# Layer 0 of a fused four-layer network: result slots, weight sets in four pairs, statistics of layer 1 ahead, sums later

## The chip, the cores and the metric

The kernel runs on one core of one Trainium2 chip. The metric is device time in microseconds. The kernel before took 2876.43 us (median of 3 runs, 2876.21 to 2878.43). The engines are named as in the profile: PE is TensorE's matmul, PEld its weight load, DVE is VectorE, ACT is ScalarE, POOL is GpSimd, SP is SyncE. SP and POOL issue almost all transfers here. [...]

## The reference

The input is 1024 images of 16 x 16 points with 16 channels, in fp32. Four layers follow one another, each of the form `x = x + f(gn(x))`, with a group norm of 8 groups of 2 channels over all points of an image:

```python
x = x + _L0_conv_ref(_gn(x), core0, core1, core2)          # tensor-train matrix of 4096 x 4096
x = x + _L1_conv_ref(_gn(x), conv1, conv2, fc0, fc1, 1)    # cellular automaton step
x = x + _L2_conv_ref(_gn(x), filters, bias)                # 3 x 3 convolution
x = x + _L3_conv_ref(_gn(x), ...)                          # a second automaton step
```

Layer 0 multiplies each image, taken as a vector of 4096, by a matrix that three small cores define. In a step of the automaton, a depthwise pair of 3 x 3 filters and the channels themselves go through two dense layers (48 to 128, ReLU, 128 to 16); a mask from 3 x 3 maxima of one channel is applied. The group norm needs, for each image and group, a mean, a variance and one over its root.

## The kernel before, in words

The batch is handled as two chunks of 512 images. Two large tiles in SBUF, `XN[0]` and `XN[1]` (names in the trace: xn), each of 128 partitions x 16384 values, hold what is being worked on. Images and results between layers stand in DRAM: `xf` is the running x of a chunk by channel and line, `xr` the raw input by line, `xb` normed blocks.

**Layer 0** is a matrix product of 4 x 4 blocks with two chunks, computed by a table of 26 outer products (`OUTER`), taken in 13 pairs, numbered 0 to 12 here (called phases in the code). A pair has 4 units (one for each quarter q of the output), so that there are 52 units. A unit has 7 inner products (`INNER`) in two half-steps each, 14 steps of 4 matmuls of 128 x 256 (L1482). Pair p works on tile `XN[p % 2]`: X in columns 0 to 8191 and three combined sums E in 8192 to 14335, both read by all its units. Around the matmuls a unit has: `build` of the weights of the next unit (matmuls L1386, copies by ACT L1391), sums of weights by DVE (`mix`, L1416), ACT copies of the first results into a result tile r (L1524, L1526) and DVE adds into it (L1518, L1528), and `store` of the unit before, at step 1: results that are added in DRAM go through POOL with an accumulating transfer (L1459), the first ones through SP (L1461). For r, units 0 to 3 and the later odd ones use one buffer (`r`), the later even ones the end of `XN[0]`.

Beside each pair run other steps, spread over the pair's steps by a small planner (`run`): a list of (cost, step) entries and of pauses, with a start and an end as shares of the pair. An entry gets its due place from the costs and pauses before it, and is emitted behind the step of the pair that has reached this place. So the planner only sets the order on each engine; nothing in it waits for a clock. These are:

- `part_steps(j)` (L1160 to L1240): loads, four of 1 MB on SP, and sums for pair j, beside pair j - 1. Pieces of 512 KB go through a ring of four buffers (`t4`), fetched two ahead. The same ring serves negated results (`neg`).
- `combined(j)` (L1131): ten DVE operations that make pair j's sums E and change X. They stand at the end of pair j - 1, or, for pairs in `late` (1, 4, 6), between the first steps of pair j itself.
- The two sets of weights of the automaton steps, `nca_weights` (L262 to L404), in columns 8192 to 14335 of `XN[0]`, beside pairs 3 and 5: many small transfers on POOL, small matmuls (L287 to L311), zero fills, and then 11 folds: `make` is four small matmuls (L392) and four ACT copies (L398) into one of three buffers, `send` stores that buffer in DRAM in small pieces, half of them on SP and half on POOL (L404).
- `residual_steps` (L1266): 32 accumulating transfers of 512 KB, raw input into `xf`, on POOL, beside pairs 4 to 9.
- The convolution's weights, beside pair 7.
- `mean_ahead` (L900 to L916), beside pair 10: the means of layer 1's norm for chunk 0, from pieces of `xf` by DVE sums (L903), a matmul over channels, an ACT copy and a store to `means`.

Beside pair 12 the result of layer 0 for chunk 0 is loaded into `XN[1]` and normed there: means are loaded and subtracted (L727), squares (ACT L712) are summed (DVE L694), a matmul gives the variance (L862), roots follow for three quarters (L767 to L778), a matmul spreads them (L874), and DVE multiplies. The last quarter is finished beside the first half of layer 1 (`layer_nca`, PE lines L1889 and L1718).

Of the kernel before, what the change touches and what calls it, by code (L numbers as in the profile page):

```python
# [10 lines left out]
F32 = mybir.dt.float32  # L11
# [10 lines left out]
P = 128  # L22
# [83 lines left out]
def conv_preact_kernel(ctx: ExitStack, tc: tile.TileContext, a: dict, out: bass.AP):  # L106
# [121 lines left out]
    def nca_weights(pre, room):  # L228
# [6 lines left out]
        L["pack"] = dram.tile([P, 833], F32, tag=pre + "pk", name=pre + "pk")  # L235

# [79 lines left out]
        def xpats():  # L316
            xw = pk[:, 0:512].rearrange("p (n k) -> p n k", n=4)
            for n, pat in enumerate(XPATS):
                for v, s in enumerate(pat):
                    if s is not None:  # L320
                        G.dma_start(xw[16 * v : 16 * v + 16, n], fz[s, 1 : S + 1])
            for g in range(1, 4):
                G.dma_start(pk[32 * g : 32 * g + 32, 0:513], pk[0:32, 0:513])
            G.dma_start(L["pack"], pk)

# [43 lines left out]
        def fold(n):  # L369

            steps = []
            for f in range(2):
# [38 lines left out]
                steps += [make, send]  # L411
            return steps

        steps = [inputs, dense0, bias_lines, bias_rows, dense1, taps, order, xpats]
        return L, steps + [x for n in range(len(TERMS)) for x in fold(n)]


# [401 lines left out]
    def paced(parts, st):  # L819

        def begin():
            st["t"], st["q"] = parts[0](), parts[1]()

        def add():
            V.tensor_tensor(st["t"], st["t"], st["q"], ALU.add)

        def last():
            st["s"] = work([P, NB], "s", "s2s")  # L830
            V.tensor_tensor(st["s"], st["t"][:, 0], st["t"][:, 1], ALU.add)

        steps = [(2, begin), (1.2, add)]
        for part in parts[2:]:
            steps += [1.5, (1, lambda part=part: st.update(q=part())), (1.2, add)]
        return steps + [(0.8, last)]

    def parts_cw(X, on_act, paced_from=4):
# [3 lines left out]
        for q in range(4):  # L842
# [6 lines left out]
            if q < paced_from:  # L849
                N["sq"].append(centred(subs, more2))  # L850
            else:
                s2.clear()
                N["sq"].append(subs + paced(squares(X, l0, 8, on_act), s2))
# [31 lines left out]
    def alone(N, q):  # L885

        return (
            N["sums"][q] + [3, N["mean"][q], 1, N["held"][q], 1] + N["sq"][q]
            + [3, N["var"][q], 1, N["keep"][q]]
        )  # L890

    means = dram.tile([4, P, NB], F32, tag="means", name="means")

    def mean_ahead(q):

        st = {}

# [3 lines left out]

        def add(w):
            V.tensor_tensor(st[0], st[0], st[w], ALU.add)  # L903

        def last():
            st["s"] = work([P, NB], "s", "s1s")
            V.tensor_tensor(st["s"], st[0][:, 0], st[0][:, 1], ALU.add)
# [5 lines left out]
        def keep():  # L913
            st["m"] = work([P, NB], "s", "m")
            A.copy(st["m"], st["p"])
            nc.sync.dma_start(means[q], st["m"])  # L916

        steps = [(0, lambda: load(0)), (0, lambda: load(2)), 4]
        for w in (2, 4, 6):
            if w < 6:  # L920
                steps.append((0, lambda w=w: load(w + 2)))
            steps.append((1.2, lambda w=w: add(w)))
        return steps + [(0.8, last), 2, (0.6, mean), 1, (0, keep)]

    def apart(N, q):

        def mean():
            N["st"]["m", q] = work([P, NB], "s", "m")
            nc.sync.dma_start(N["st"]["m", q], means[q])

        return [(0, mean), 3] + N["sq"][q] + [5, N["var"][q], 1, N["keep"][q]]
# [213 lines left out]
    def part_steps(j):  # L1145
# [25 lines left out]

# [34 lines left out]
        if todo:  # L1206
            steps += [(0, lambda: fetch(0)), (0, lambda: fetch(1)), 3]
# [909 lines left out]
```

## Time and profile before

| what | value |
|---|---|
| median of the runs | 2876.43 us |
| the profiled execution | 2877.63 us, of which the span of its instructions 2875.9 us |
| PE / DVE / ACT / POOL busy | 2722.2 / 1987.6 / 1267.0 / 510.7 us |
| layer 0, pairs 0 to 12 | 46.9 to 1678.4 us |
| pair 3, pair 5 | 148.4 us, 160.2 us |
| pair 7, pair 9 | 108.4 us, 114.3 us |
| pair 10, 11, 12 | 115.8, 107.2, 123.8 us |
| layer 1, first and second chunk | 244.6 us, 237.0 us |

Times in the trace count from the start of the span. In a table of stretches each row is one stretch, with its length, the busy time and the instruction count of each engine, the granted TensorE clock as a share, the busy share of the 16 DMA engines, and GB/s. In a list of waits a row names the engine and line that waited, whom it waited for, the total in us, how often, and the longest. In groups of instructions a row has the busy time, the mean of one in ns, and the idle time ahead of them.

### The profile page before, as it was taken

How to read it: one execution, taken by the hardware profiler on the slowest of the kernel's cores; microseconds unless marked ns; L12 is line 12 of the kernel's file. 1: busy time of each engine (PE TensorE's matmuls, PEld its weight loads, DVE VectorE, ACT ScalarE, POOL GpSimd, SP SyncE). 2: the span in 40 equal slices, each digit the busy share in tenths (PEclk: the TensorE clock that was granted, in tenths of full speed). 3: DMA queues.
4: the chain of work that ended last, by engine and by line, in shares of the span. 5: the costliest groups of instructions: out<-in, count | busy, mean ns of one | idle time of the engine just before them, and what ended most of it. 6: DMA issues, size and time to landing. Idle time of an engine off the chain costs nothing.

```text
span 2875.9 us, 48113 instructions
## 1 busy us (share of the span) xinstructions
PE 2722.2 (95%) x19342; PEld 1776.3 (62%) x19342; DVE 1987.6 (69%) x2420; ACT 1267.0 (44%) x2140; POOL 510.7 (18%) x662
## 2 busy tenths in 40 slices
PE   6888899799979999999999999999999999999997
PEld 5677788578757888888888743333333333334444
DVE  8476667666747867756666788857877776766654
ACT  3223322242233222222222346666778657676664
POOL 2000012642452142121011011111112221110000
PEclk8989999899989999999999999999999999999998
DMA  6566576899888788897667365455566867454665
GB/s 249 175 222 251 192 211 147 198 222 186 217 178 215 173 183 190 191 227 186 167 173 187 76 160 105 96 128 154 108 145 137 190 101 195 101 101 104 172 176 202
DMA packets 254558, 488.29 MB, mean 170 GB/s; under 512 B 28708, under 2 KB 96344, under 8 KB 245120
## 3 DMA queue, kind: packets, MB, share of 16 engines
q1 hardware_dynamic: 172240, 328.16, 34.7%
q0 software_dynamic: 81904, 156.93, 32.2%
q8 instruction: 153, 2.51, 0.3%
q14 instruction: 69, 0.57, 0.1%
q10 hardware_dynamic: 192, 0.13, 0.0%
HBM read 268.98 MB, written 221.11 MB: 170 GB/s over the span
## 4 chain that ended last, share of the span: by engine, by line
PE 78%; DVE 7%; DMA 7%; issue 2%; POOL 2%; ACT 1%; SPq 1%; DVEq 0%; ACTq 0%; POOLq 0%
PE po L1482 36%; PE ph L1889 20%; PE po L1718 8%; PE po L1573 5%; PE pw L1386 5%; DMA xf<-r 1%; DMA xn<-in_x_dram 1%; DMA L_conv_wy<-xn 1%; PE po L1582 1%; DVE xn L1102 1%; DVE xn L727 1%; PE ptin L1020 1%; DMA m<-means 1%; PE ptx L1782 1%; DVE xn L1131 1%
## 5 line engine op out<-in xcount | busy, mean ns | idle before, releaser
L1482 PE MATMUL po<-xn,s 128*128 128x256 f32 x3328 | 768.5, 388 | 22.1 <-DVE s L1416 9.5
L1892 ACT ACTIVATE hid<-ph,pack 128x512 f32<-128x512 f32 (+1 forms) x1040 | 640.9, 684 | 308.3 <-PE ph L1889 245.7
L1482 PEld LDWEIGHTS po<-xn,s 128*128 128x128 f32 x3328 | 637.3, 194 | 130.7 <-issue 24.1
L1482 PE MATMUL po<-xn,w 128*128 128x256 f32 x2496 | 573.2, 385 | 4.0 <-DVE xn L1131 4.0
L1482 PEld LDWEIGHTS po<-xn,w 128*128 128x128 f32 x2496 | 471.6, 192 | 86.5 <-issue 13.8
L1889 PE MATMUL ph<-xn,wq 32*128 32x512 f32 (+1 forms) x3752 | 515.6, 590 | 4.0 <-DVE u L1730 3.6
L1391 ACT COPY w<-pw 128x512 f32<-128x512 f32 x416 | 213.6, 601 | 479.7 <-PE pw L1386 373.8
L1889 PEld LDWEIGHTS ph<-xn,wq 32*128 32x128 f32 x3752 | 233.2, 184 | 229.5 <-issue 208.6
L1416 DVE TENSOR_TENSOR s<-w 128x1024 f32<-128x1024 f32 x208 | 251.5, 1218 | 82.1 <-PE po L1482 78.9
L1889 PE MATMUL ph<-xn,pack 32*128 32x512 f32 x1288 | 278.4, 621 | 8.5 <-DVE u L1730 3.9
L1718 PE MATMUL po<-hid,pack 128*32 128x512 f32 (+1 forms) x2080 | 260.5, 596 | 0.7 <-ACT hid L1892 0.5
L727 DVE TENSOR_TENSOR xn<-xn,m 128x1024 f32<-128x1024 f32 x160 | 187.8, 1218 | 42.8 <-ACT m L750 36.1
L1730 DVE SCALAR_TENSOR_TENSOR u<-po,pack,xn 128x512 f32<-128x512 f32 (+1 forms) x130 | 96.3, 741 | 158.2 <-PE po L1718 157.2
L1772 POOL DMA_DIRECT2D xf<-u x96 | 82.6, 860 | 632.1 <-DVE u L1770 602.8
L1386 PE MATMUL pw<-R,gq 32*128 32x128 f32 x3328 | 150.1, 290 | 47.0 <-ACT xn L398 30.6
L1889 PEld LDWEIGHTS ph<-xn,pack 32*128 32x128 f32 x1288 | 116.8, 187 | 96.6 <-issue 69.7
L1386 PEld LDWEIGHTS pw<-R,gq 32*128 32x128 f32 x3328 | 121.1, 192 | 82.3 <-issue 40.8
L1518 DVE TENSOR_TENSOR r<-r,po 128x1024 f32<-128x1024 f32 x84 | 102.2, 1217 | 92.0 <-PE po L1482 70.5
L1718 PEld LDWEIGHTS po<-hid,pack 128*32 128x32 f32 x2080 | 54.7, 109 | 179.8 <-ACT hid L1892 85.5
L1573 PE MATMUL po<-xn,convw 128*128 128x512 f32 x368 | 163.6, 598 | 0.0
L1518 DVE TENSOR_TENSOR xn<-xn,po 128x1024 f32<-128x1024 f32 x72 | 87.6, 1217 | 106.1 <-PE po L1482 95.8
L1131 DVE TENSOR_TENSOR xn<-xn 128x1024 f32<-128x1024 f32 x130 | 154.3, 1217 | 7.1 <-DMA xn<-xb 7.1
(213 smaller groups left out, 2761.8 us busy)
## 6 DMA issues: line engine op xcount, KB each, us to landing
xn<-xf SPq DMA_DIRECT2D x96, 512.0 KB
xn<-xb SPq DMA_DIRECT2D x36, 1024.0 KB
wq<-L_conv_wy SPq DMA_DIRECT2D x192, 192.0 KB
piece<-xb SPq DMA_DIRECT2D x64, 512.0 KB
xf<-xn POOLq DMA_DIRECT2D x48, 512.0 KB, 10.3
xf<-neg POOLq DMA_DIRECT2D x48, 512.0 KB, 8.8
xf<-r POOLq DMA_DIRECT2D x48, 512.0 KB, 12.3
xf<-u POOLq DMA_DIRECT2D x96, 256.0 KB, 4.2
```

The source lines that it names most:

```text
L727: V.tensor_tensor(part, part, m().unsqueeze(1).broadcast_to([P, 2, NB]), op)
L1131: V.tensor_tensor(out, y, z, f)
L1386: T.matmul(pw[r][:, v, i], g[rows, P * (2 * v + i) : P * (2 * v + i) + P], R[rows, k], start=k == 0, stop=k == len(gs) - 1,)
L1391: A.copy(w.rearrange("p b s t m -> p (b s t) m")[:, :, 32 * r : 32 * r + 32].rearrange("p k (v o) -> p v k o", v=2), pw[r].rearrange("p v ...
L1416: V.tensor_tensor(t.rearrange("p s t m -> p (s t m)"), x, y, f)
L1482: T.matmul(po[:, i], matrix(u, what)[:, i, t], x, start=t == 0, stop=t == 3)
L1518: V.tensor_tensor(part, part, po.unsqueeze(2).broadcast_to([P, 2, 2, 256]), ALU.add)
L1573: T.matmul(st["po", h][wh], conv["fw"][:, y], X[:, 16 * wh + h + y - 1], start=y == max(0, 1 - h), stop=y == min(2, S - h),)
L1718: T.matmul(po[32 * j : 32 * j + 32], nca["w1"][:, v], hid[j], start=v == 0, stop=v == 1)
L1730: V.scalar_tensor_tensor(u, po, nca["b1"], X[:, 8 * q + w2, cols(hf)], ALU.add, ALU.add)
L1889: T.matmul(ph, w, x, start=k == 0, stop=k == len(tiles) - 1)
L1892: A.activation(h, ph, AF.Relu, bias=nca["bt"][:, r : r + 1])
```

## The change

It has five parts, all in layer 0.

1. Results of pair 0: unit 1 takes as r columns 6144 to 8191 of `XN[1]`, unit 3 columns 14336 to 16383; units 0 and 2 keep the buffer. The load of pair 1 that goes to columns 6144 to 8191 is issued behind the norm steps of its first half.
2. The weight sets: `nca_weights` now returns the preparation and the folds apart. Preparation ends with three copies and a store of the packed values and of the fold's two operands (`kept`); the folds begin with a reload (`again`). Preparation runs beside pairs 3 and 7, the folds beside pairs 5 and 9, with other pauses. The convolution's weights move from pair 7 to pair 8.
3. `combined` also stands in its own pair for 2, 8, 10 and 12.
4. Residual adds are spread over pairs 2 to 12 (3, 3, 3, 2, 2, 2, 2, 3, 4, 4, 4).
5. Layer 1's norm of chunk 0: beside pair 10 the means of four quarters and the variances of two; beside pair 11 the variances of the other two, the roots and their spread, stored to `roots`. A piece is summed by two DVE operations of half the size (before: one of the whole size). For a variance, a piece is loaded, its mean subtracted by DVE, squared by ACT and summed. Beside pair 12 only subtraction and multiplication remain, for all four quarters, with means and roots loaded; nothing of it is left for layer 1's first half. Pieces of `part_steps(12)` are no longer fetched ahead, and those of pair 11 one ahead.

```diff
@@ nca_weights
+        def store():
             G.dma_start(L["pack"], pk)
+            G.dma_start(kept[:, 0:NB], fs)
+            G.dma_start(kept[:, NB:], tp.rearrange("p n f m -> p (n f m)"))
+
+        def again():
+            nc.sync.dma_start(fs, kept[:, 0:NB])
+            nc.sync.dma_start(tp.rearrange("p n f m -> p (n f m)"), kept[:, NB:])
...
-        steps = [inputs, dense0, bias_lines, bias_rows, dense1, taps, order, xpats]
-        return L, steps + [x for n in range(len(TERMS)) for x in fold(n)]
+        steps = [
+            inputs, 14, dense0, 12, bias_lines, 3, bias_rows, 3, dense1, taps, 12, xpats, 10, order,
+            copies, 14, store,
+        ]
+        folds = [again, 8]
+        for make, send in (x for n in range(len(TERMS)) for x in fold(n)):
+            folds += [make, (1, send), 2.5]
+        return L, steps, folds
@@ ahead(kind, q, root), in place of mean_ahead(q) and apart(N, q)
+        def centre(w):
+            V.tensor_tensor(
+                st[w], st[w], st["m"].unsqueeze(1).broadcast_to([P, 2, NB]), ALU.subtract
+            )
+            A.activation(st[w], st[w], AF.Square)
+
         def add(w):
-            V.tensor_tensor(st[0], st[0], st[w], ALU.add)
+            x = st.pop(w)
+            if w == 0:
+                st["s"] = work([P, NB], "s", "s1s")
+                V.tensor_tensor(st["s"], x[:, 0], x[:, 1], ALU.add)
+                return
+            for i in range(2):
+                V.tensor_tensor(st["s"], st["s"], x[:, i], ALU.add)
...
+        steps = [(0, fetch)] if kind else []
+        steps += [(0, lambda: load(0)), (0, lambda: load(2)), 4]
+        for w in (0, 2, 4, 6):
+            steps += centred_too(w) + [(1.3 if w else 0.7, lambda w=w: add(w))]
+            if w < 4:
+                steps.append((0, lambda w=w: load(w + 4)))
+            steps.append(1)
+        if kind:
+            return steps + [1, (0.6, var), 1, (0.4, keep_var)]
+        return steps + [1, (0.6, mean), 1, (0, keep_mean)]
@@ part_steps
+        deep = {NP - 2: 1, NP - 1: 0}.get(j, 2)
...
-        steps = [(0, lambda p=p, wh=wh: load(p, wh)) for p in range(2) for wh in range(2)] + [8]
+        loads = [(0, lambda p=p, wh=wh: load(p, wh)) for p in range(2) for wh in range(2)]
+        steps = loads[: 3 if j == 1 else 4] + [8]
         for p in range(2):
+            if p == 1 and j == 1:
+                steps.append(loads[3])
...
-            steps.append((0, lambda i=i: fetch(i + 2)))
+            steps.append((0, lambda i=i: fetch(i + deep)))
+            if not deep:
+                steps.append(4)
@@ pieces
-                    if k == 0 and (u < 4 or u % 2):
+                    at = {1: (1, 6144), 3: (1, 14336)}.get(u)
+                    if u > 3 and u % 2 == 0:
+                        at = (0, 14336)
+                    if k == 0 and not at:
                         st["r", u] = work([P, 2, 2, NB], "r", "r0")
@@ the schedule
-        late = (1, 4, 6)
+        late = (1, 2, 4, 6, 8, 10, 12)
...
-        residual = {4: (0, 0, 5), 5: (0, 5, 10), 6: (0, 10, 16), 7: (1, 0, 5), 8: (1, 5, 10), 9: (1, 10, 16)}
+        aside = {3: set1, 5: fold1, 7: set3, 9: fold3}
+        aside[8] = [lambda: conv.update(s=conv_weights()), 60, lambda: conv["s"]()]
+        aside[10] = [x for at in ((0, 0), (0, 1), (0, 2), (0, 3), (1, 0), (1, 1)) for x in ahead(*at, root)]
+        aside[11] = ahead(1, 2, root) + ahead(1, 3, root) + roots_ahead(root)
+        share = {2: 3, 3: 3, 4: 3, 5: 2, 6: 2, 7: 2, 8: 2, 9: 3, 10: 4, 11: 4, 12: 4}
...
-            if j in (3, 5):
-                spans.append((paused(make1 if j == 3 else make3), 0.0, 0.97))
...
+            if j in aside:
+                spans.append((aside[j], 0.02, 0.97))
+            spans.append((terms[: share[j]], 0.05, 0.95))
...
-            steps_of(phases[NP - 1]), 107, load_cw(X0, xf[0]) + [put(L1)], (bg, 0.12, 1.0), by=0.25
+            steps_of(phases[NP - 1]), 107, load_cw(X0, xf[0]) + [put(L1)], (bg, 0.15, 0.98),
+            (terms, 0.05, 0.95), by=0.4,
...
-            layer_nca(X0, 0, 1, L1), 250, load_cw(X1, xf[1]), (last, 0.0, 0.21),
-            (norm_cw(X1, False), 0.23, 1.0), by=0.3,
+            layer_nca(X0, 0, 1, L1), 250, load_cw(X1, xf[1]), (norm_cw(X1, False), 0.2, 1.0), by=0.3,
```

## The prediction

> **What bounds the kernel now.** I read the slices first: TensorE is busy nearly everywhere, at full clock, except in the first third, at pairs 0, 3 and 5 of layer 0 and at its end. So the next view is the table of stretches, cut at every 448th record of L1482 (one pair of products). Columns: length, then busy us of PE, PEld, DVE, ACT, POOL, then the granted clock, the DMA share and GB/s.
>
> ```profile
> 46.90:213.20 166.30, 141.18 (x960) 117.67 (x961) 107.74 (x100) 42.82 (x112) 0.56 (x1) 0.90 0.54 178
> ...
> 474.10:622.50 148.40, 128.66 (x805) 98.31 (x804) 89.16 (x105) 52.88 (x98) 85.61 (x139) 0.93 0.91 204
> 622.50:731.70 109.20, 109.18 (x770) 94.04 (x769) 81.08 (x81) 29.02 (x52) 28.95 (x27) 1.00 0.92 208
> 731.70:891.90 160.20, 138.89 (x998) 106.74 (x997) 87.17 (x104) 52.63 (x97) 81.70 (x139) 0.90 0.85 189
> 891.90:1000.00 108.10, 107.31 (x706) 92.19 (x705) 100.41 (x95) 26.16 (x49) 18.01 (x16) 1.00 0.80 196
> ...
> 1331.60:1447.40 115.80, 115.80 (x905) 99.06 (x904) 72.25 (x72) 28.10 (x53) 11.02 (x9) 1.00 0.66 187
> 1447.40:1554.60 107.20, 107.20 (x706) 92.41 (x706) 72.32 (x70) 25.11 (x48) 13.47 (x11) 1.00 0.63 154
> 1554.60:1678.40 123.80, 114.55 (x653) 92.66 (x651) 93.39 (x101) 34.93 (x56) 11.00 (x9) 0.97 0.49 126
> ```
>
> The rows are pairs 0, 3, 4, 5, 6, 10, 11, 12. A pair whose weights come from one gather takes 107.2 (pair 11), that is 26.8 a unit; a unit that builds from two gathers takes 28.6 (pair 9: 114.3). Pairs 6, 10 and 11 are PE-bound; pairs 3 and 5 lie 41 and 48 us above that floor, pair 0 59, pair 12 17. The waits by engine, first TensorE's in pair 0, then in pair 3, pair 5 and pair 12, then ACT's in pair 3, say why:
>
> ```profile
> PE ptin L1020 <- ACT lines L1030: 9.3, 2, 9.0
> PE pw L1386 <- ACT xn L662: 7.3, 1, 7.3
> PE po L1482 <- ACT r L1526: 4.5, 1, 4.5
> ```
>
> ```profile
> PE pw L1386 <- ACT xn L398: 16.4, 2, 13.3
> ```
>
> ```profile
> PE pw L1386 <- ACT xn L398: 14.2, 1, 14.2
> PE L_conv_pe L392 <- POOL xn L350: 5.5, 1, 5.5
> ```
>
> ```profile
> PE po L1482 <- DVE s L1416: 6.8, 1, 6.8
> PE pr L874 <- DVE r L778: 2.4, 1, 2.4
> ```
>
> ```profile
> ACT xn L398 <- DMA L_conv_wy<-xn: 22.9, 3, 11.3
> ```
>
> and ACT's in pair 0:
>
> ```profile
> ACT r L1524 <- DMA xf<-r: 37.4, 3, 14.3
> ```
>
> Pairs 3 and 5: the fold's copies (L398) wait until the stores of the fold three before have left its buffer; those stores stood in POOL's queue behind the end of the set's preparation (first L404 on POOL at 557.7; TensorE stood from 553.3 to 566.6). ACT's copies for the next weights queue behind, and TensorE waits for them. Pair 0: all three of TensorE's waits begin with ACT's first copy into the results: the results have one buffer, freed only when stored.
>
> **The skill.** "TensorE: Matmul & The Clock Gate", HAM oscillation: idle gaps above some 3.4 us lower the clock. The trace agrees: 0.90, 0.93, 0.90 in the three pairs with long gaps, and L1482 is busy 112.9, 104.1 and 108.1 us there against 99.1 in pair 10; a gap removed returns more than its length. "VectorE: DVE Perf Modes", The TRN2 errata: an fp32 tensor_tensor takes (N+151)/0.96 ns, 691 for 512 elements; the trace has 685, and 1217 to 1221 for 1024, so many half-size adds are dear. "DMA: Bandwidth & Descriptors", Issuing engines are not separate DMA queues: all transfers share 16 engines; pair 10's first unit stands at a DMA share of 0.97.
>
> **The change, part by part, in us of the profiled execution.**
>
> Pair 3 loses the 11 folds (44 matmuls at L392: 12.2 busy) and the wait for them; the set's own PE work stays (L287 to L311: 3.1). 107.2 + 3.1 + 1.7 of small waits = 112: -36.
>
> Pair 5 loses the second set (3.1) and takes the first set's folds. Three units at 28.6 and one at 26.8 are 112.6; + 12.2 + 1.7 = 126.5: -34. Folds now stand 8.3 us apart instead of 5.1. Once POOL's backlog was gone (from 832 on), pair 5 ran folds and residual adds with no PE wait over 0.7, so no stall is expected. Pair 7 gets the second set: 108.4 to 112, +3.5. Pair 9 gets its folds: +12.
>
> Pairs 4 and 8: the set's copies and store are now last in pairs 3 and 7, and in POOL's order behind eight zero fills and a unit's six accumulating stores (8 to 12 us to landing). DVE's sums of pair 4 and 8, moved into those pairs, overwrite that room and wait for these stores; behind them stand the mixes. The sums themselves are free where tried (pair 4: 109.2 with them), but unit 0 then has no slack (pair 6: 0.8 lost). 0 to 8 each; I take 3: +6. The reload of the parts (two transfers on SP's queue) is hidden by 8 us of pause. The convolution's weights move from pair 7 to 8 with 42 small transfers on POOL and seven short DVE operations, hidden by the 20 us that DVE idles in each.
>
> Pair 0: waits of 20.8 go, as units 1 and 3 write into the input tile; staging for L662, freed by its own stores, takes perhaps 3 back, and the clock returns some 3: -20. The delayed fourth load of pair 1 comes some 10 us after unit 1's store, which landed in 5 to 6. Pair 1 to 2: the 4.2 us before pair 2's first matmul, with DVE still in pair 2's sums, goes as these are later: -5. Residual adds before pair 4 cost POOL some 8 us of waiting each (L1266), three in each of pairs 2 and 3: hidden, as POOL idled 63 us of pair 3 and 84 us sufficed it for the whole set in pair 5 with three such adds among it.
>
> Pair 10. PE: 115.8 + two variance matmuls at 1.03 = 117.9. DVE: 72.3, less 12 piece sums (14.6) and four halves (2.7), plus 8 subtractions (9.8), 42 half adds at 0.685 (28.8), ten sums of pair 10 itself (12.2) and two at L870's 0.68 (1.4) = 107.2. That fits only without waits. Before, the four sets of pieces cost DVE waits:
>
> ```profile
> DVE piece L903 <- DMA piece<-xf: 16.3, 5, 7.3
> ```
>
> 4 us a set. Six sets: 24.5, so 131.7, 14 over. And it is uneven. Unit 0: 12.7 of its own + 12.2 + two sets at 4.8 = 34.5 against 28.6, with pieces behind 4.2 MB of loads: 13 lost. Units 1 and 2 two each. Unit 3 without its set is 20.7, + 11.4 = 32 against 27.6, + 3 of landing: 8. Together +25. PE's mean and variance matmuls wait in line for those sums, so the lag stops TensorE directly. Bounds: +2 (all hidden) to +40.
>
> Pair 11. PE 107.2 + 2.1 + four root spreads at 1.13 = 113.8. DVE 72.3 - 12.2 + 9.8 + 9.6 + 1.4 + 8.3 (roots, at the rates of L774 to L778) = 89.2; pair 12's eight pieces are now fetched just before use, 4 us of pause against 5.5 to landing. I take 8 of stall: +15 (bounds +6.5 and +25).
>
> Pair 12 loses three variances and three spreads (6.5) and the roots; subtract and multiply cost DVE 32 x 1.217 = 39 for 51 removed, plus 12.2 of sums: 94 of 114. The means' fetch again queues behind loads: 6.5 of wait. 107.2 + 6.5 = 113.7: -10. First half of layer 1: loses a variance, a spread and DVE's quarter; it has 8.8 us of PE waits for DVE against 1.1 in the next half: -4.
>
> Sum: -36 - 34 + 3.5 + 12 + 6 - 20 - 5 + 25 + 15 - 10 - 4 = -47.5. The profiled execution took 2877.6 (span 2875.9), so 2830; the median, 1.2 lower, gives 2829, and I say 2830.
>
> **The rivals.**
> (a) DVE absorbs the ahead work: pairs 10 and 11 pay PE work alone, +8.5 for +40: 2798. Speaking for it: pair 6 had 100.4 of DVE in 108.1 and full DMA in its first units and lost 0.8. Against: nothing there waited on freshly issued pieces.
> (b) The fold's stall stays, since accumulating stores and residuals still hold POOL's queue: pairs 5 and 9 lose 14 to 16 each plus 5 of clock, +40: 2870. For it: POOL waited 2 to 4 us at L404 for xf stores. Against: three buffers at 8.3 us cover 25 us, and landing at L404 has a median of 3.6 (at most 19.9).
> (c) Slower: exposed landings in pairs 10 and 11. Every two pieces are waited for in full, 12 times in pair 10 (six sets of four) and 12 in pair 11 (two sets of four and eight single ones): at 6 us, 107.2 + 72 - 117.9 = 61 and 89.2 + 72 - 113.8 = 47, with PE's 8.5 some 117 against the 87.5 gained elsewhere: 2906. It decides from 4.8 us a wait on. For it: one set took 10.7 from issue (1395) to use. Against: the next took 5.5 (1376.5 to 1382.0), of which DVE waited 3.7, then 0.9 for the second two.
> (d) Pair 0 gains nothing, the DVE (62 of 78 us busy in its last units) being next: 2850, inside the range.
>
> **The numbers.** Main course, with (d): 0.60, its own range 2806 to 2858; (a) 0.18; (b) 0.14; (c) 0.08. Range for 8 in 10: 2796 to 2872. A measurement of this kernel tells about 0.2% (5.8 us) from no change. Faster: 0.60 + 0.18 + 0.11 of (b) = 0.89; same 0.03; slower 0.08.
>
> **What would show it.** Pairs 3, 5, 7, 9 at 112, 126, 112, 126 with no TensorE wait on the fold's copies over 2 us and clock 1.00: right. No ACT wait on xf stores in pair 0. Pair 10 near 141 and pair 11 near 122, TensorE waiting there for the means' and variances' sums, DVE for pieces. I am wrong if a stall at L398's successor returns, if the starts of pairs 4 and 8 lose over 8 us to the store of the set, or if pairs 10 and 11 run at PE's pace.

## The result, and the profile after

The changed kernel takes 2871.43 us (median of 14 runs, 2865.1 to 2873.84), the kernel before beside it 2876.28 us (14 runs): ratio 0.9983, 95% interval 0.9974 to 0.9991. It is faster, by 4.9 us where 46 were forecast: the interval just excludes no change, and the prediction had put what such a measurement can tell apart at 5.8 us. The profiled execution took 2871.3 us, span 2869.6 against 2875.9.

The pairs, from the first matmul L1538 (before: L1482) of one to that of the next, in us; "forecast" is the step of the prediction, "missed by" is measured less forecast:

| part | before | after | change | forecast | missed by |
|---|---|---|---|---|---|
| pair 0 | 166.4 | 140.2 | -26.2 | -20 | -6.2 |
| pairs 1 and 2 | 260.9 | 253.1 | -7.7 | -5 | -2.7 |
| pair 3 | 148.4 | 124.9 | -23.5 | -36 | +12.5 |
| pairs 4 and 8 | 218.0 | 251.1 | +33.1 | +6 | +27.1 |
| pair 5 | 160.2 | 130.2 | -30.0 | -34 | +4.0 |
| pair 6 | 108.1 | 108.1 | 0.0 | 0 | 0 |
| pair 7 | 108.4 | 110.6 | +2.2 | +3.5 | -1.3 |
| pair 9 | 114.3 | 132.0 | +17.8 | +12 | +5.8 |
| pair 10 | 115.9 | 158.3 | +42.4 | +25 | +17.4 |
| pair 11 | 107.1 | 125.4 | +18.3 | +15 | +3.3 |
| pair 12 | 123.8 | 105.7 | -18.1 | -10 | -8.1 |
| behind layer 0 | 1197.6 | 1182.8 | -14.8 | -4 | -10.8 |

The table of stretches of the kernel after, cut at the starts of the pairs (columns as in the prediction); the rows are pairs 0, 3, 4, 5, 8, 9, 10, 11, 12:

```profile
47.10:187.20 140.10, 133.60 (x960) 112.03 (x960) 107.30 (x100) 43.26 (x112) 1.24 (x3) 0.97 0.64 212
...
440.40:565.30 124.90, 115.84 (x718) 96.70 (x717) 89.55 (x105) 29.33 (x54) 71.56 (x101) 0.96 0.88 196
565.30:697.60 132.30, 113.60 (x769) 96.77 (x768) 81.07 (x81) 29.02 (x52) 29.64 (x29) 0.91 0.86 199
697.60:827.80 130.20, 128.84 (x986) 100.72 (x985) 80.78 (x76) 52.64 (x96) 44.30 (x58) 0.99 0.87 208
...
1046.50:1165.30 118.80, 112.37 (x769) 96.01 (x768) 89.57 (x94) 27.73 (x51) 42.77 (x62) 0.97 0.80 194
1165.30:1297.40 132.10, 130.74 (x1050) 102.53 (x1050) 63.91 (x64) 52.48 (x96) 41.80 (x56) 0.99 0.82 197
1297.40:1455.60 158.20, 129.44 (x909) 104.27 (x908) 104.40 (x117) 36.22 (x61) 14.84 (x13) 0.91 0.66 182
1455.60:1581.10 125.50, 118.18 (x718) 95.56 (x718) 87.98 (x103) 36.05 (x61) 17.07 (x15) 0.97 0.73 184
1581.10:1686.80 105.70, 104.88 (x641) 90.20 (x639) 91.93 (x84) 21.00 (x40) 14.62 (x13) 1.00 0.71 180
```

Pairs 0 and 5 have lost their holes, that is the time in which TensorE stands, as forecast (length less PE busy: 6.5 and 1.4, from 25 and 21). New holes stand in pairs 4 (18.7), 8 (6.4) and 10 (28.8), and pair 3 keeps 9.1. And the clock column shows a second price: where there are holes the clock is 0.91 to 0.97, and PE is busy longer with the same matmuls.

**Pair 3.** TensorE waits there for weights that VectorE mixes, and for an ACT copy:

```profile
PE po L1538 <- DVE s L1469: 4.9, 2, 3.9
PE po L1538 <- ACT xn L1582: 3.9, 1, 3.9
```

**Pair 4.** TensorE's waits there, then ACT's and VectorE's longest ahead of them:

```profile
PE po L1538 <- ACT xn L1582: 11.2, 1, 11.2
PE po L1538 <- DMA xf<-neg: 7.5, 1, 7.5
```

```profile
ACT neg L1498 <- DMA xf<-neg: 17.3, 1, 17.3
ACT xn L1580 <- DMA xf<-xn: 8.2, 1, 8.2
```

```profile
598.11 1.23 DVE L1178 TENSOR_TENSOR xn<-xn 128x1024 f32<-128x1024 f32 x1 [24.59 <-DMA L_conv_kp<-xn]
```

These are two chains. In the first, ACT stands 17.3 and 8.2 us until result stores of pair 3 have landed and left their buffers, and TensorE stands 11.2 us for its copies. In the second, VectorE's sums of pair 4 (L1178) stand 24.6 us for the store of the kept parts; the sum ends at 599.3 and TensorE goes on at 599.4, so its second wait, for which the view names a store, was for this sum. Where the stores are, POOL's timeline shows (start, duration, line; in brackets the idle time ahead and what ended it):

```profile
572.77 0.50 POOL L326 DMA_DIRECT2D xn<-xn  x1 [2.73 <-DMA xf<-neg]
589.45 0.58 POOL L329 DMA_DIRECT2D L_conv_pk<-xn  x1 [16.18 <-DMA xn<-xn]
590.02 0.55 POOL L330 DMA_DIRECT2D L_conv_kp<-xn  x1
590.55 0.54 POOL L331 DMA_DIRECT2D L_conv_kp<-xn  x1
591.09 5.00 POOL L1512 DMA_DIRECT2D xf<-neg  x4
```

The set's last copy (L326) is issued at 572.8, behind six result stores of 512 KB (557 to 567) that took 17 and 21 us to land (the medians of xf<-neg and xf<-xn). POOL waits 16.2 us for the copies ahead of the set's stores, and the results of pair 3's last unit (L1512) stand behind those in the same queue until 591. The DMA engines are full here, at 209 GB/s, before pair 4's loads are issued (a share can exceed 1, as a transfer is counted whole where it starts):

```profile
570.00:575.00 5.00, 5.00 (x25) 4.38 (x25) 3.52 (x4) 0.00 (x0) 0.54 (x2) 1.00 1.13 209
```

```profile
579.26 3.34 SPq L1207 DMA_DIRECT2D xn<-xb  x4
```

The loads (L1207, 4 MB) come so late because they stand in SP's queue behind a store (L1514) that waited 19.9 us for ACT. Pair 8 has the second chain in small: VectorE waits 10.5 us, TensorE 5.9.

**Pair 10.** TensorE waits for the sums ahead of the means and variances:

```profile
PE pmean L806 <- DVE s1s L909: 19.0, 3, 9.3
PE pvar L922 <- DVE s1s L909: 5.9, 2, 4.9
```

One turn of it on SP's and then on DVE's timeline:

```profile
1349.77 0.32 SPq L918 DMA_DIRECT2D means<-m  x1
1350.49 2.56 SPq L890 DMA_DIRECT2D piece<-xf  x4
```

```profile
1359.53 0.69 DVE L906 TENSOR_TENSOR s1s<-piece 128x512 f32<-128x512 f32 x1 [10.17 <-DMA piece<-xf]
```

The reads of the next quarter (L890) stand in SP's queue behind the store of the means of the one before (L918), which waits for ACT's copy, which waits for the matmul, which waits for the sum. So the quarters don't overlap: store 1349.8, reads 1350.5, first sum 1359.5. The units of pair 10 took 41.6, 44.6, 36.0 and 36.1 us (before 28.6, 29.4, 30.3, 27.6).

**Behind layer 0** all of the gain lies in the first 100 us. First the kernel before, then the kernel after:

```profile
1678.40:1778.40 100.00, 92.33 (x664) 36.28 (x668) 80.22 (x107) 64.20 (x103) 11.11 (x12) 0.93 0.61 156
```

```profile
1686.80:1786.80 100.00, 97.72 (x786) 38.53 (x790) 68.79 (x86) 68.99 (x112) 13.36 (x15) 1.00 0.66 165
```

Of PE's waits for DVE some 6 us went, and with them the low clock (0.93 to 1.00).

### The profile page after: what moved, and what is told of

It reads as the page before. It is cut to its first block, busy times and chain, and to the rows that moved or that the text cites. A ratio compares the mean times of both kernels' runs of the same rounds, so it can differ in the third digit from the quotient of the medians.

```text
span 2869.6 us, 48201 instructions
## 1 busy us (share of the span) xinstructions
PE 2722.4 (95%) x19342; PEld 1771.9 (62%) x19342; DVE 1999.9 (70%) x2440; ACT 1268.9 (44%) x2139; POOL 525.8 (18%) x666
## 4 chain that ended last, share of the span: by engine, by line
PE 72%; DMA 10%; DVE 9%; issue 5%; POOL 2%; ACT 1%; SPq 1%; DVEq 0%; POOLq 0%; ACTq 0%
PE po L1538 30%; PE ph L1945 20%; PE po L1774 8%; PE po L1629 5%; PE pw L1439 4%; DMA xf<-r 1%; DMA piece<-xf 1%; DMA xn<-xn 1%; DVE xn L1178 1%; DMA xf<-neg 1%; DVE xn L1149 1%; DMA xn<-in_x_dram 1%; DMA xf<-xr 1%; PE po L1638 1%; PE L_conv_pe L403 1%
## 5 line engine op out<-in xcount | busy, mean ns | idle before, releaser
L1538 PE MATMUL po<-xn,s 128*128 128x256 f32 x3328 | 774.7, 390 | 48.9 <-DVE s L1469 17.8
L1538 PEld LDWEIGHTS po<-xn,s 128*128 128x128 f32 x3328 | 639.7, 195 | 165.7 <-issue 24.7
L1538 PE MATMUL po<-xn,w 128*128 128x256 f32 x2496 | 574.3, 385 | 4.5 <-DVE xn L1178 4.5
L1538 PEld LDWEIGHTS po<-xn,w 128*128 128x128 f32 x2496 | 471.9, 192 | 86.4 <-issue 10.3
L1178 DVE TENSOR_TENSOR xn<-xn 128x1024 f32<-128x1024 f32 x130 | 154.2, 1219 | 35.1 <-DMA L_conv_kp<-xn 35.1
L744 DVE TENSOR_TENSOR xn<-xn,m 128x1024 f32<-128x1024 f32 x128 | 150.3, 1219 | 34.7 <-ACT m L767 34.6
L1574 DVE TENSOR_TENSOR r<-r,po 128x1024 f32<-128x1024 f32 x78 | 95.0, 1218 | 69.5 <-PE po L1538 60.4
L1217 DVE TENSOR_TENSOR xn<-xn,piece 128x1024 f32<-128x1024 f32 x96 | 116.2, 1220 | 34.8 <-DMA piece<-xb 34.8
```

Of the source, the lines that this page charges most:

```text
L744: V.tensor_tensor(part, part, m().unsqueeze(1).broadcast_to([P, 2, NB]), op)
L1178: V.tensor_tensor(out, y, z, f)
L1217: V.tensor_tensor(y, y, x(), ALU.add if sign > 0 else ALU.subtract)
L1538: T.matmul(po[:, i], matrix(u, what)[:, i, t], x, start=t == 0, stop=t == 3)
```

## Experiments

Each is timed against the kernel before (2874 to 2875 us in the same sittings; 2876 in that of the changed kernel). The pairs are read from one profiled execution of each. Pair 10 has the same instructions in the changed kernel, set_early, share_later, share_none and negs_a, and there it takes 155.9 to 159.2, so a difference of some 3 us in a pair says nothing. The text put on record ahead of each run sets a theory A against a rival B, with what either would show. In us:

| kernel | median, ratio to before (interval) | 3 | 4 | 8 | 10 | 11 | 12 | behind layer 0 |
|---|---|---|---|---|---|---|---|---|
| before | | 148.4 | 109.1 | 108.9 | 115.9 | 107.1 | 123.8 | 1197.6 |
| changed | 2871.4, 0.9983 (0.9974 to 0.9991) | 124.9 | 132.3 | 118.8 | 158.3 | 125.4 | 105.7 | 1182.8 |
| late_old | 2878.1, 1.0009 (0.9998 to 1.0019) | 122.5 | 134.5 | 121.3 | 155.9 | 125.8 | 105.4 | 1185.8 |
| pieces_first | 2844.4, 0.9889 (0.9864 to 0.9913) | 122.6 | 134.9 | 119.8 | 137.8 | 121.3 | 105.8 | 1185.5 |
| reads_only | 2858.6, 0.9946 (0.9927 to 0.9964) | 123.5 | 132.3 | 119.0 | 145.8 | 126.0 | 105.1 | 1183.9 |
| ahead_undone | 2849.1, 0.9907 (0.9891 to 0.9923) | 122.9 | 133.9 | 119.8 | 119.7 | 107.1 | 124.6 | 1196.1 |
| set_early | 2857.2, 0.9936 (0.9922 to 0.9951) | 127.0 | 124.0 | 110.6 | 156.5 | 121.8 | 105.5 | 1181.9 |
| slots_only | 2850.0, 0.9915 (0.9899 to 0.9932) | 150.5 | 111.7 | 108.9 | 115.9 | 107.1 | 124.0 | 1197.1 |
| share_later | 2862.6, 0.9961 (0.9946 to 0.9976) | 124.4 | 125.3 | 117.1 | 155.9 | 126.7 | 105.4 | 1183.1 |
| share_none | 2865.0, 0.9963 (0.9953 to 0.9974) | 121.0 | 127.6 | 119.1 | 159.2 | 125.9 | 105.3 | 1183.7 |
| best_a | 2844.1, 0.9893 (0.9879 to 0.9908) | 147.6 | 111.0 | 109.5 | 135.1 | 121.1 | 105.4 | 1181.7 |
| best_b | 2850.2, 0.9913 (0.9898 to 0.9928) | 150.7 | 110.0 | 109.0 | 118.4 | 107.2 | 129.2 | 1195.4 |
| best_c | 2839.6, 0.9877 (0.9861 to 0.9894) | 140.5 | 110.1 | 110.7 | 135.7 | 121.3 | 105.5 | 1183.3 |
| set_sp | 2850.6, 0.9920 (0.9899 to 0.9942) | 154.6 | 110.3 | 109.7 | 135.2 | 118.7 | 106.0 | 1184.1 |
| best_e | 2831.1, 0.9853 (0.9832 to 0.9875) | 142.3 | 110.2 | 108.9 | 139.0 | 119.0 | 105.5 | 1185.2 |
| negs_a | 2864.5, 0.9958 (0.9943 to 0.9973) | 119.5 | 129.5 | 124.8 | 157.8 | 125.1 | 105.8 | 1182.4 |
| negs | 2835.6, 0.9864 (0.9847 to 0.9880) | 125.6 | 124.5 | 110.3 | 133.4 | 120.9 | 106.1 | 1182.0 |

### What makes pair 10 long: the load on VectorE, or the order?

The theory after the result was the serial chain through SP's queue; the rival, VectorE's load. **late_old** takes load away:

```diff
-        late = (1, 2, 4, 6, 8, 10, 12)
+        late = (1, 2, 4, 6, 8)
```

> The changed kernel with the sums of pairs 10 and 12 computed ahead again, at the end of pairs 9 and 11 (12.2 us of VectorE each), and nothing else different. Theory A, VectorE's load makes pair 10 slow: it has 92 us instead of 104 there, pair 10 falls by 10 to 18 us from 158.3, pair 12 changes little, pairs 9 and 11 grow by 0 to 5, and the time is about 2860. Rival B, the landing of the pieces and the serial order make it slow: pair 10 falls by less than 5, and the time is 2868 to 2878.

In this kernel the sums of pair 10, now in pair 9, overwrite the room from which the second set's folds still read, so those weights are not the reference's; the amount of work is the same. Its waits of TensorE in pair 10:

```profile
PE pmean L806 <- DVE s1s L909: 17.1, 3, 7.3
PE pvar L922 <- DVE s1s L909: 5.9, 2, 4.9
```

With VectorE at 94 instead of 104 us, pair 10 is 2.4 us shorter, which is within that spread, and the waits for the sums are still 23.0 (24.9 in the changed kernel). The load isn't the cause. **pieces_first** leaves the load and changes the order; it goes through the sets of pair 10 and 11 in this way (each set's last four entries are pause, matmul, pause, keep):

```diff
+            for i, ((kind, _), x) in enumerate(zip(ats, sets)):
+                out += x[3 + kind : -4] if i else x[:-4]
+                if i + 1 < len(sets):
+                    out += sets[i + 1][: 3 + ats[i + 1][0]]
+                out += x[-4:]
```

> The changed kernel with the steps of the sums ahead in another order: the first two reads of the next set are issued before the matmul, the copy and the store of the set before, and the matmul so stands some 4 us later in TensorE's order. Nothing is added or left out. Theory A, the chain is serial through SP's queue (the next reads stand behind the store of the means, which waits for the copy, which waits for the matmul): TensorE's waits for the sums (24.9 us in pair 10) fall under 8 and with them goes the loss of clock, pair 10 is 130 or less, and the time about 2845. Rival B, VectorE has too much to do (104 us and its waits) and lags anyway: the waits move from the mean's matmul to the mixes' products, pair 10 stays over 148, and the time is 2862 to 2872.

Its pair 10, by the stretches and by TensorE's waits:

```profile
1296.00:1433.70 137.70, 125.48 (x909) 102.91 (x908) 104.66 (x117) 35.98 (x61) 14.83 (x13) 0.95 0.76 209
```

```profile
PE pvar L922 <- DVE s1s L909: 5.3, 1, 5.3
...
PE pmean L806 <- DVE s1s L909: 2.1, 1, 2.1
```

VectorE does the same 104.7 us of work in 20.5 us less, and the waits for the sums fall from 24.9 to 7.4. Pair 10 ends above the 130 that was expected, as its first unit still takes 35.4 us for 28.6. **reads_only** parts the two halves of this cure: the reads go ahead of the copy and the store, the matmul stays where it was. Against pieces_first:

```diff
-                out += x[3 + kind : -4] if i else x[:-4]
+                out += x[3 + kind : -2] if i else x[:-2]
...
-                out += x[-4:]
+                out += x[-2:]
```

> The changed kernel where only the order on SP differs: the first two reads of the next set are issued ahead of the store of the means, not behind it, while the mean's matmul stands where the changed kernel has it in TensorE's order. It parts the two halves of the cure that took pair 10 from 158.3 to 137.8. Theory A, the serial chain through SP's queue is what counts: pair 10 is 144 or less, most of the cure, and the time is 2848 to 2856. Rival B, what counts is that the matmul stands just behind its sum in TensorE's order: pair 10 stays above 150, and the time is 2862 to 2872.

```profile
PE pmean L806 <- DVE s1s L909: 13.5, 3, 8.4
PE pvar L922 <- DVE s1s L909: 4.9, 1, 4.9
```

145.8: between the two expectations. SP's order is worth 12.5 of the 20.5 us, and the later place of the matmul the other 8. The first unit gains little from SP's order alone (40.0, from 41.6): its stop (8.4 us, 9.3 in the changed kernel) is not the chain's. There VectorE waited 5.8 us for the second two pieces of the first set, and the matmul stood just behind that sum. **ahead_undone** prices the part as a whole:

```diff
-        aside[10] = [x for at in ((0, 0), ..., (1, 1)) for x in ahead(*at, root)]
-        aside[11] = ahead(1, 2, root) + ahead(1, 3, root) + roots_ahead(root)
+            if j == NP - 3:
+                spans.append(([x for q in range(4) for x in mean_ahead(q)], 0.15, 0.95))
```

> The changed kernel with its last part undone: only the four means are computed ahead in pair 10 (full-size additions, two reads ahead everywhere), the variances and roots of layer 1 again in pair 12 and in the first half of layer 1. The moved sums and the residual additions stay. Theory A, the work ahead costs more than it gives back: of the +42.4, +18.3, -18.1 and -14.8 us measured in pairs 10, 11, 12 and behind layer 0, the whole returns, so pair 10 about 116 to 125, pair 11 107 to 110, pair 12 near 124, and behind layer 0 1197; the sum is -28 and the time about 2843. Rival B, the moved sums of pairs 10 and 12 or the residual additions are what slows pairs 10 and 11: they stay over 140 and 117, the gains of pair 12 and layer 1 are lost as well, and the time is 2880 or more.

Pairs 10 and 11 give back 56.9 us, pair 12 and layer 1 cost 32.2: part 5 costs 25 us net in the change's form, and in the order of pieces_first it about breaks even (2844 against 2849). Pair 10 is at 119.7 here, with the moved sums and the residual additions still in it, so that these two cost it 4 us at most.

### The set's store in pairs 4 and 8

**set_early** ends the sets of pairs 3 and 7 at 0.7 of the pair:

```diff
-                spans.append((aside[j], 0.02, 0.97))
+                spans.append((aside[j], 0.02, 0.7 if j in (3, 7) else 0.97))
```

> The changed kernel with one difference: the sets of pairs 3 and 7 are spread over 0.02 to 0.70 of their pair and not to 0.97, so that their copies and stores leave POOL's queue before the loads of the next pair start. Theory A, the store of the set is late: pair 4 falls from 132.3 to 112 or less and pair 8 from 118.8 to 111 or less, together some 26 us, VectorE's wait for the kept parts (24.6 and 10.5 us) goes, and the time is about 2846. Rival B, the two pairs lose their time to the sums that were moved into them, whatever the set does: they stay within 5 us of 132 and 119, and the time is 2866 to 2872. Rival C, the wait only moves: the copies now stand in pair 3's third and fourth unit in front of POOL's result stores, pair 3 grows from 124.9 to 138 or more, and the time is some 2860.

Pair 8 is down by 8.2 to 110.6, but pair 7 up by 5.2, since the first wait for the set's inputs now shows (3.5 us). In pair 4, VectorE's wait for the kept parts is gone; instead TensorE's and VectorE's waits are

```profile
PE po L1538 <- DVE xn L1178: 5.5, 1, 5.5
PE po L1538 <- ACT xn L1582: 4.9, 1, 4.9
```

```profile
DVE xn L1217 <- DMA xn<-xb: 10.0, 1, 10.0
```

So the set's store explains 8 of pair 4's 23 us (TensorE's second wait, 7.5, is gone) and most of pair 8's 10. ACT's waits for result stores have shrunk, to 11.9 and 7.2, but not gone. In **best_a** the sets end at 0.50, with the order of pieces_first:

> The changed kernel with both cures: the sets spread over 0.02 to 0.50 of pairs 3 and 7, and the next pieces' reads ahead of the means' matmul and store. Theory A, at 0.70 the result stores of pair 3's third unit still stood behind the set's copies and left POOL (563 to 567 us) as the next loads began (569): with 0.50 they leave before, pair 4 falls from 124.0 to 115 or less, pairs 10 and 11 are 138 and 121, and the time is 2844 - 24 = 2820. Rival B, pair 4's loss in its first unit comes from something else (full DMA engines): pair 4 stays above 121, and the time is about 2830. Below 2835 both causes act apart from each other.

Pair 4 falls to 111.0, and pair 3 grows from 127.0 to 147.6. Its waits of TensorE in pair 3:

```profile
PE L_conv_pt L288 <- DMA xn<-in_L_conv_fc_w_dram: 10.1, 1, 10.1
PE po L1538 <- ACT xn L1582: 7.1, 1, 7.1
PE po L1538 <- ACT r L1582: 6.6, 1, 6.6
PE po L1538 <- DVE s L1469: 5.5, 1, 5.5
```

The first is the inputs' landing, which the shorter pause no longer covers; of the others that for r is new, and those for ACT's copy into xn and for VectorE's mix were 3.9 and 4.9 in the changed kernel. Pair 4 fell as theory A had it, but the gain didn't come (2844.1 us, where 2820 or 2830 was expected), and as pair 3 is 20 us longer its stores also had more time to land: that the earlier set alone freed pair 4 is not shown. **best_b**, with part 5 undone as in ahead_undone in place of the order, shows the same in pairs 3 and 4 (150.7 and 110.0):

> As the run before it in the sets (0.02 to 0.50 of pairs 3 and 7), but with the last part undone (four means ahead in pair 10, variances and roots of layer 1 in pair 12 and layer 1) in place of the new order. If the work ahead in its new order is worth having, this one is slower by about what the two single runs differed, 5 us: 2825 with theory A of that run and 2835 with B. If the two cures get in each other's way, this one is the faster.

### Part 1 alone

In **slots_only** the kernel before gets two hunks of the diff: the results' places, and the fourth load of pair 1.

> The kernel before with part 1 of the change alone: results of units 1 and 3 in free places of the input tiles, and the fourth part load of pair 1 later. Theory A, the gain of pair 0 comes from the results' places: pair 0 falls from 166.4 to about 140, pair 1 by 0 to 7, every later pair stays within 1 us, and the time is 2843 to 2850. Rival B, the gain of pair 0 needs the later sums and the other parts too: pair 0 stays above 155, and the time is 2862 or more.

Pair 0 is 140.3; every later pair is within 3 us of before. This part alone is worth 24.6 us (ratio 0.9915), and by it alone the kernel is some 20 us faster than with the whole change (0.9983). So the other four parts together cost about what part 1 gains, less 5 us.

### Pairs 3 and 4: amount of transfers, or waits?

Pairs 3 and 4 together took 257.6 us before and 257.2 after. First the residual additions:

```diff
-        share = {2: 3, 3: 3, 4: 3, 5: 2, 6: 2, 7: 2, 8: 2, 9: 3, 10: 4, 11: 4, 12: 4}
+        share = {2: 0, 3: 0, 4: 4, 5: 3, 6: 3, 7: 3, 8: 3, 9: 4, 10: 4, 11: 4, 12: 4}
```

> The changed kernel with the six residual additions of pairs 2 and 3 moved on into pairs 4 to 9, one more in each. Theory A, they delay POOL's queue in pair 3 (each is waited for there, and the result stores, and with them the buffers of the pieces, stand behind them): pair 3 falls from 124.9 to 118 or less, VectorE's waits for pieces there (9.8 us) go, pairs 4 to 9 grow by 0 to 2 each, and the time is about 2866. Rival B, the set's own small transfers do it: pair 3 stays over 121, and the time is 2868 to 2878.

Pair 3 hardly moved (rival B held there, though not in the time), pair 4 fell by 7.0, and the sum by 7.5. **best_c** joins this with set_early and pieces_first:

> The changed kernel with the sets spread over 0.02 to 0.70 of pairs 3 and 7, the next reads and the later matmul in pairs 10 and 11, and the residual additions of pairs 2 and 3 moved to pairs 4 to 9. If the three cures add up: 2844.4 - 14.2 - 8.8 = 2821. If the residual additions in pair 4 and the sets at 0.70 remove the same waits of pair 4 (it fell by 8.3 with the one and by 7.0 with the other), only one of the two counts there: 2828 to 2831. Pair 3 stays at 122 to 127 in both.

The sum of the pairs is 250.6, no less than with set_early (251.0) or share_later (249.7) alone: 140.5 and 110.1 in place of 124.4 and 125.3. In **set_sp** the set's small transfers go from POOL's queue to SP's:

> As the run before it, but 40-odd small transfers of each set (taps, patterns, copies, stores) are issued on SP's queue and no longer on POOL's. Theory A, pairs 3 and 4 lose their time because these stand in POOL's queue ahead of the result stores, whose landing frees the buffers of the pieces: pair 3 falls to 118 or less and pair 4 to 115 or less, some 10 to 15 us less than the run before it. Rival B, the same transfers hold up whatever queue they stand in (on SP's they wait for VectorE's copies ahead of the weights' and pieces' reads): pair 3 stays above 123 or grows, and the time is no shorter than that of the run before it.

That made pair 3 longer by 14 (VectorE waited 34.5 us for pieces there): rival B. Then **share_none** (on the changed kernel) and **best_e** (with the order of pieces_first and the sets of set_early) take all residual additions out of pairs 2 to 5 (pairs 6, 7 and 8 have 5, 5 and 6):

> The changed kernel with all residual additions of pairs 2 to 5 (3, 3, 3 and 2) moved into pairs 6, 7 and 8, which have 5, 5 and 6. Theory A, pairs 3 and 4 together are bound by the DMA engines: their sum was 257.6 us before and 257.2 after, at shares of 0.91 and 0.92 before and 0.88 and 0.86 after, and one accumulating store of 512 KB takes some 3.4 us of all 16 engines there (154 us for 45 of them); six fewer make 20 us, so the sum falls to 237 to 243 and the time to 2852 to 2858, with 0 to 2 us lost in each of pairs 6 to 8. Rival B, the order in the queues and the waits for landing make the length, not the amount: the two fewer of the run with six moved gave 7.5 us by order alone, the sum stays above 246, and the time is 2862 or more.

> As the run before it, and with the sets at 0.02 to 0.70 and the next reads and the later matmul in pairs 10 and 11. With theory A: the four additions that the best version so far still had in pair 4 make 13 us of DMA, so pairs 3 and 4 fall from 250.6 to about 238 and the time from 2839.6 to about 2828. With rival B they stay above 247, and the time is 2836 to 2842.

From pair 3's start to the end of pair 4's first unit, in turn the kernel before, the changed one, share_none and best_e:

```profile
474.10:649.50 175.40, 155.64 (x982) 121.25 (x980) 114.53 (x129) 60.22 (x111) 95.26 (x147) 0.94 0.92 216
```

```profile
440.40:615.40 175.00, 147.24 (x893) 122.36 (x892) 114.88 (x129) 36.45 (x67) 84.54 (x114) 0.90 0.93 216
```

```profile
439.70:606.00 166.30, 146.03 (x893) 121.17 (x891) 114.80 (x129) 36.66 (x67) 80.99 (x110) 0.92 0.91 215
```

```profile
441.30:611.60 170.30, 141.75 (x893) 118.94 (x893) 114.02 (x129) 36.98 (x67) 70.80 (x110) 0.92 0.84 204
```

The change took 11 folds of PE work out of this stretch (155.6 to 147.2) and its length stayed. Before and after, the DMA engines were busy 0.92 and 0.93 of it, 161 and 163 us. Taking some 11 us of transfers out (share_none) shortened it by 8.7; with 20 us less (best_e, whose profile is of its slowest execution, 2839.0 us for a median of 2831.1) it was 4.7 shorter only. And set_early, which takes no transfer out, is 6.1 shorter with a DMA share of 0.94 (168.9 us). Rival B held for the pairs in both runs (248.6 and 252.4): the amount alone doesn't set the length. **negs_a** (on the changed kernel) and **negs** (on best_c) move three negatives of pair 3 out of the buffers that they share with the pieces:

```diff
+            spare = {12: [13193], 13: [13193, 8576]}.get(u, [])
...
-                    have[c] = t = work([P, 2, NB], "t4", "neg")
+                    at = spare.pop(0) if 12 <= u < 14 and spare else None
+                    if at:
+                        t = flats[0][:, at : at + 1024].rearrange("p (s b) -> p s b", s=2)
+                    else:
+                        t = work([P, 2, NB], "t4", "neg")
+                    have[c] = t
```

> The same three negatives moved in the changed kernel itself. Theory A: its pair 3 (124.9, where 112 was forecast) falls to 118 or less, as the waits for pieces (9.8 us) and the two stops of 3.9 us behind them go; pair 4 still waits for the set's store and stays at 128 to 134; the time is about 2864. Rival B: pair 3 stays above 122 and the time is 2868 to 2874.

> The best version with two negatives of pair 3's second unit and one of its first kept in places of the set's room that are free by then (4 KB each), not in the four buffers that they share with the pieces; nothing else differs. Theory A, pair 3 stands because the reads of the pieces wait for a buffer until negatives have been stored (SP waited 27.2 us there for that) and VectorE's mixes queue behind the pieces (16.3 us, TensorE 15.6): pair 3 falls from 140.5 to 122 or less, pair 4 stays at 110 to 112, and the time is about 2821. Rival B, the landing itself is slow, whenever the reads are issued: pair 3 stays above 133 and the time above 2832.

One of these places still held operands of the set's bias rows, so that the first set's values aren't the reference's; the work is the same. In best_c, pair 3 stood for this (waits of SP's queue and of VectorE there):

```profile
SPq L1255 <- DMA xf<-neg: 27.2, 5, 13.9
```

```profile
DVE xn L1217 <- DMA piece<-xb: 17.0, 2, 16.3
```

In negs VectorE's wait for pieces in pair 3 is gone and the pair falls by 15, to 125.6; in negs_a it falls to 119.5, from 122.5 to 124.9 in the five kernels that share the changed kernel's pair 3. The pieces did wait for buffers that stores had not yet freed. But pair 4 of negs is 14.4 longer:

```profile
PE po L1544 <- ACT xn L1588: 6.1, 1, 6.1
PE po L1544 <- DVE xn L1178: 5.8, 1, 5.8
```

The sum is 250.1 for 250.6: the stop has moved into pair 4, where ACT again waits for pair 3's result stores (13.0 and 7.4 us). Taking out a wait (set_early 251.0, negs_a 249.0) or transfers (share_later 249.7, share_none 248.6) brings the sum of the pairs from 257 to some 250, and doing several of these at once (best_c 250.6, negs 250.1, best_e 252.4) brings it no further. What sets the 250 us is not settled.

best_e is the fastest that ran, at 0.9853 (0.9832 to 0.9875) of before; best_c's interval overlaps with it.

## Why the prediction was right or wrong

The sign was right and the range held by a hair (2871.4 of 2796 to 2872); the size was wrong: -4.9 where -46 were forecast, and the main course's own range, 2806 to 2858, was missed. The sign rests on part 1 (-24.6 in slots_only), as the other parts together cost some 20. And 2871 is next to rival (b)'s 2870 by chance: the stall that (b) named did not come. Three steps failed: the store of the set (pairs 4 and 8), the quarters in pair 10, and small waits in pair 3; the clock made each of them dearer.

**Pair 0, pair 1 to 2: right**, a little too careful (-33.9 for -25). No ACT wait for stores of results is left in pair 0, and slots_only, with pair 0 at 140.3, shows that part 1 brings the gain. Rival (d) fell.

**Pairs 5, 7, 9: right in kind.** No wait for a fold exceeds 0.7 us (rival (b) fell). Pairs 5 and 9 are 4 and 6 us over: PE was busy 128.8 and 130.7 for the 124.8 and 126.5 worked out. The clock, 0.99 in both, is 1.7 us of that in pair 5 (kernels in which it did not fall there took 128.5); where the rest comes from is open.

**Pair 3: a term too small.** The folds' stall went, but "107.2 + 3.1 + 1.7" counts 1.7 us of small waits. Measured are 9.1 us of holes and 115.8 of PE busy for the 110.3 worked out; these two make the 12.5 missed. negs_a points to one of these waits: pieces that waited for buffers. A warning stood in the table of before, a DMA share of 0.91 and 0.92 in pairs 3 and 4. After the change the engines were busy 224 us there (124.9 x 0.88 + 132.3 x 0.86), as long as the 221 to 224 us that the forecast gave both pairs. That this forbade the forecast is argued and not shown: best_e, with some 20 us less of it, still took 252.4 for both.

**Pairs 4 and 8: the step that failed by most.** "0 to 8 each; I take 3": measured +23.2 and +9.9. The prediction's own sign of being wrong, over 8 us in these starts, came. The mechanism was named (POOL's order, VectorE's sums behind the store), and its size was taken too small. Missing were the 16.2 us for which POOL stood for the copies ahead of the store, as they landed behind six result stores, and ACT's waits for these result stores, which stopped TensorE for 11.2 us. set_early shows the first for pair 8 and for 8 us of pair 4; the second is read from the trace and has no experiment of its own.

**Pair 10: the right mechanism with one term too small.** Unit 0 lost 13.0 and unit 3 8.5, as worked out (13 and 8). "Units 1 and 2 two each" were 15.2 and 5.7. Of the 17.4 us missed, 11.5 are PE busy longer than worked out (129.4 for 117.9) and 5.8 are holes (28.8 for the 23 that the forecast of 141 left). I had counted a set's landing 4 us at a time and not seen that the store of the means, in SP's queue between two sets, makes each set's reads wait for the whole chain of the set before. pieces_first and reads_only show this; late_old shows that VectorE's 104 us was not it. Rival (c) named exposed landings, and its price, 12 waits in full, was too high: VectorE waited 29.5 us for pieces in pair 10.

**The clock: a term that was missing.** The prediction's main sum let the clock return where holes went, and charged nothing where holes came (only rival (b) had 5 us for it). PE busy less the PE work that was worked out, or that was measured before, is 11.5 us in pair 10, and 5.5, 4.4, 3.6 and 4.4 in pairs 3, 4, 8 and 11: 29 us, beside 41 missed in the sum of all parts. That this is the clock for the most part is an estimate: what it took off full speed there, one less the clock column times the length, is 14, 5, 12, 4 and 4 us, holes included.

**Pair 12 and layer 1: right in sign, too small** (-33 for -14). The 6.5 us for the means' fetch didn't appear (pair 12: 105.7, at full clock, with 104.9 of PE work where the sum had 107.2), and in layer 1 the clock's return was again not counted.

## What to carry to other kernels

Before a stage is forecast at its engine's floor, multiply its DMA share by its length: where that comes near the forecast, as it did for pairs 3 and 4, small waits can't be put at next to nothing. When a store is put last in a stage, add what stands ahead of it in its queue, and ask which buffers the stores of the stage itself still hold. When reads for the next turn stand behind a store on one queue, the turns don't overlap, whatever the load: issue the reads first (12 us of 158 here, and 20 with the matmul behind its sum moved later, without any work removed). Charge each new stop of TensorE with the clock too.

## What the runs showed of the hardware

The price of a stop, in three stretches of pair 10 in the changed kernel (the stop of 9.2 us, 4 us behind it, the next 4):

```profile
1313.60:1322.80 9.20, 0.00 (x0) 0.00 (x1) 7.27 (x9) 0.00 (x0) 0.00 (x0) 0.73 1.10 239
1322.80:1326.80 4.00, 4.00 (x7) 2.49 (x8) 4.00 (x4) 0.59 (x1) 0.00 (x0) 0.50 0.23 62
1326.80:1330.80 4.00, 4.00 (x44) 3.23 (x45) 2.42 (x4) 0.00 (x0) 0.00 (x0) 0.84 1.01 312
```

The granted clock falls during the stop (0.73 on its average) and is half behind it, for some 5 us as estimated from these means. This agrees with the Trainium skill, "TensorE: Matmul & The Clock Gate", HAM oscillation, where a wait longer than the idle window lets the matmuls behind it start throttled. What I had not expected is that the clock also falls without a long stop: in pair 5, where weights of 32 matmul rows are built and a fold with 9 rows follows behind an idle 0.7 us,

```profile
790.00:792.00 2.00, 2.00 (x6) 1.55 (x6) 0.00 (x0) 0.62 (x2) 0.38 (x1) 0.50 0.33 44
```

and pair 5, with the same matmuls, took either 130.2 or 128.5 us (in nine and in six of the fifteen profiled kernels that have the first set's folds there, the changed one among them). In pair 6 of the changed kernel an accumulating store cost the DMA engines about twice as much for a MB as the other transfers: 6.29 MB in POOL's queue, all of it such stores, took 34.5% of the engines' time, and 12.67 MB of other transfers 33.4%, so 5.9 against 2.8 us.
